# A gated recurrent layer: the first turned inputs by transposing loads instead of TensorE

## The chip, the core and the metric

The kernel runs on one core of a Trainium2 chip. The metric is the device time of one execution in microseconds. The page and the timelines give times from the start of the profiled span. Engines are named as in the profile: PE is TensorE (PEld its weight loads), DVE is VectorE, ACT is ScalarE, POOL is GpSimd, SP is SyncE, which here only issues transfers.

## The reference

```python
def step(h, inp):                       # 128 steps, batch 64, width 512
    x_t, prop = inp
    comb = concatenate([x_t, h], -1)
    z = sigmoid(comb @ Wz + bz)
    r = sigmoid(comb @ Wr + br)
    comb2 = concatenate([x_t, r * h], -1)
    h_cand = tanh(comb2 @ Wh + bh)
    h_new = (1.0 - z) * h + z * h_cand
    h_next = where(prop, tanh(h_new @ Wp + bp), h_new)   # prop: every 4th step
    return h_next, h_new
out = x + (h_new of every step)
```

All is float32. x is 64 x 128 x 512, each gate's weights are 1024 x 512: the upper half meets x, the lower half h.

## The kernel before, in words

**Layout.** The 128 partitions hold two halves of the 512 columns (`s` = 0, 1) for the 64 rows of the batch. A product with a 512 x 512 matrix is four products `k`, each issued once per half: eight matmuls with a stationary operand of 128 x 64 and a moving one of 128 x 256 (`products`, L188). The stationary operand has the contracted columns on the partitions, so h, r*h and x must be turned before they are used.

**A turn on PE** (`turn`, L206 to 222). A float32 is treated as two 16-bit words. For each of two column chunks, four transposes of bf16 halves go to the PSUM tile `turn`, and one copy by DVE or ACT (L204) puts the words side by side again. One step's x takes eight such transposes and two copies (`turn_x`, L237), the copies on ACT.

**A turn by a load.** x of later steps comes in groups `g` of four steps: a load into `xs` (`load_xs`), a copy on POOL that puts the low and high words apart into `xw` (`words_x`, L249, one instruction per step), one transposing load on SP's queue from `xw` to `xv` for the whole group (`planes_x`, L259), and a copy on ACT per step that joins the words in `xT` (`join_x`, L269). In this kernel that begins with group 4, that is with x of step 16. x of steps 0 to 7 comes from `xr`, that of steps 8 to 15 from `early[2]` and `early[3]`, which borrow buffers of the pool `mb` and are loaded at the start.

**The loop over t** (L624) issues, for each step: the R product, sigmoid (L675) and rh = r*h (L676, DVE), the Z product with the turns of rh inside it, z, 1 - z and keep, the H product, tanh (L719), two DVE operations to the new h, and the turns of h. Every fourth step has one more product with Wp and turns `hprop` in place of h. ACT also copies the part that comes from x into the PSUM slot of each gate for the next step (`seed`, L393; L395 in the profile). The program gives each engine its instructions in the order in which the code names them, under a manual schedule, and an engine works through them in that order.

**What fills PE meanwhile.** The products with x do not depend on h. They lie in a list `queue`; `fill(n)` takes n units from it, at places given by hand (`PLACES`, `places`). For x of steps 2 to 7 a unit is a plain product (`plain`, twelve units a step; its result is read by DVE at L420 and L425). From group 2 on the products of eight steps are computed in batches by a fast matrix scheme of 7 x 7 products over sums of x and of weights: `batches`, `batch`, with end copies on ACT (L506, L507, L514) and additions on DVE (L508, L509, L515 to L517), run by `read_out`.

**Sums for the batches.** Sums of weights are made at the start: on DVE `sum_outer` (L311 to L313) in step 0, `sum_outer_1` (L317, two instructions) at the end of step 2, `sum_inner_1` (L325, three instructions) in step 3 ahead of rh, and one more set at the end of step 3 (L320 to L325); the others on POOL. Sums of x are made on POOL: `sum_raw12` and `sum_raw4` (four instructions each), `sum_s12` and `sum_s34` (six each: two for `o`, L352/L353 and L360/L361, and four for `s`, L334 to L337). For group 2, `sum_raw12` stands at the end of step 2, `sum_s12` in step 3 after the R product, `sum_s34` at the end of step 3. POOL also adds h to x for the output in every step (L805).

**Where the turns of x stand in steps 0 to 5.** After the R product x of steps 2, 5, 8, 11, 13, 15 (L663); between fill and the H product in steps 0 to 2 x of 3, 6, 9 (L709); at the end of steps 0 to 4 x of 4, 7, 10, 12, 14 (L755). At two places in a step, after `seed(R, t + 1)` and after keep, stands `join(n)` (L653).

Of the kernel before, what the change touches and what calls it, by code (L numbers as in the profile page):

```python
# [11 lines left out]
U16 = mybir.dt.uint16  # L12
# [5 lines left out]
def kernel(  # L18
# [29 lines left out]
    nc = tc.nc  # L48
# [81 lines left out]
    early = {}  # L130
# [25 lines left out]
    def cut(ps):  # L156
        return ps.rearrange("p (c n) -> p c n", c=C)
# [39 lines left out]
    def product(ps, lT, w, k, start=False):  # L197
        s0, c0 = divmod(k, C)
        products(ps, lT[:, c0, ts(s0, B)], lambda s: w[:, k, ts(s, N)], start)
# [3 lines left out]
    def copy(eng, dst, src):  # L203
        (eng.copy if eng is nc.scalar else eng.tensor_copy)(dst, src)  # L204

    def turn(src, dst, c, name, eng):  # L206


        pt = turn_ps[c][:, :P].bitcast(BF16).rearrange("p (w n) -> p w n", w=2)
        for s in range(S):  # L210
            words = src[:, c * P + s * B : c * P + (s + 1) * B].bitcast(BF16)
            for w in range(2):
                nc.tensor.transpose(  # L213
                    pt[s * B : (s + 1) * B, w, :],
                    words.rearrange("p (n w) -> p w n", w=2)[:, w, :],
                    ident16,
                )
        copy(
            eng,
            dst[:, c, :].bitcast(U16).rearrange("p (n w) -> p n w", w=2),  # L220
            pt.bitcast(U16).rearrange("p w n -> p n w"),
        )
# [6 lines left out]
    xs = {}  # L229
    xw = {}  # L230
    xv = {}

    def new_xT(g):
        if g not in xT:
            xT[g] = xtp.tile([P, Q4, C, P], F32, tag="xT", name=f"xT_{g}")

    def turn_x(t, eng=nc.scalar):  # L237
        g, i = divmod(t, Q4)
        new_xT(g)
        src = xr[g] if g < 2 else early[g]  # L240
        for c in range(C):
            turn(src[:, i, :], xT[g][:, i], c, f"xT_{t}", eng)
# [6 lines left out]
    def words_x(g, i):  # L249

        if g * Q4 >= T:
            return
        if g not in xw:
            xw[g] = one.tile([P, Q4, 2, N], U16, tag="xw", name=f"xw_{g}")
        nc.gpsimd.tensor_copy(
            xw[g][:, i], xs[g][:, i, :].bitcast(U16).rearrange("p (n w) -> p w n", w=2)
        )

    def planes_x(g):  # L259

        if g * Q4 >= T:
            return
        xv[g] = one.tile([P, Q4, 2, C, P], U16, tag="xv", name=f"xv_{g}")
        nc.sync.dma_start_transpose(
            out=xv[g].rearrange("p t w c n -> p (t w c) n"),
            in_=xw[g].rearrange("p t w n -> p (t w n)"),
        )

    def join_x(g, i):  # L269

        if g * Q4 >= T:
            return
        new_xT(g)
        nc.scalar.copy(  # L274
            xT[g][:, i].bitcast(U16).rearrange("p c (n w) -> p w c n", w=2), xv[g][:, i]
        )
# [17 lines left out]
    def inner(i, ka, na):  # L294
        return OPERAND[i](ka)[:, :, :, ts(na, P // 2)]
# [13 lines left out]
    def sum_outer():  # L309
        for ka in range(S):  # L310
            nc.vector.tensor_sub(tw[3][:, ka], outer(1, 1, ka), outer(0, 1, ka))  # L311
            nc.vector.tensor_add(tw[2][:, ka], tw[3][:, ka], outer(0, 0, ka))
            nc.vector.tensor_sub(tw[4][:, ka], outer(1, 0, ka), tw[2][:, ka])  # L313
# [5 lines left out]
    def sum_inner(i, eng):  # L319
        eng.tensor_sub(tt[:, i - 1, 1], inner(i, 1, 1), inner(i, 0, 1))  # L320
        eng.tensor_add(tt[:, i - 1, 0], tt[:, i - 1, 1], inner(i, 0, 0))
        eng.tensor_sub(tt[:, i - 1, 2], inner(i, 1, 0), tt[:, i - 1, 0])

    def sum_inner_1(i, eng):
        eng.tensor_sub(inner(i, 0, 1), inner(i, 0, 1), inner(i, 0, 0))  # L325
# [67 lines left out]
    def seed(i, t):  # L393
        if t < T:
            nc.scalar.copy(cut(slots[i]), G[t][:, :, i, :])  # L395
# [5 lines left out]
    def fill(n):  # L401
        for _ in range(min(n, len(queue))):
            unit, end = queue.pop(0)
            unit()
            if end is not None:
                pending.append(end)

    def read_out():
        while pending:
            pending.pop(0)()  # L410
# [213 lines left out]
    for t in range(T):  # L624
        g, j = divmod(t, Q4)
        prop = j == CHUNK - 1 and t < T - 1
        last = t == T - 1
        pair, u = divmod(t - 3, 8)
# [22 lines left out]
            assert len(queue) == 7  # L651

        def join(n):  # L653
            if pair >= 0 and u in (5, 6):
                join_x(even + 2, 2 * (u - 5) + n)
            elif pair >= 1 and u in (1, 3):
                join_x(odd, u - 1 + n)


        for k in ORDER:  # L660
            product(slots[R], hT, wh[R], k)
        if t < 6:
            turn_x((2, 5, 8, 11, 13, 15)[t])  # L663
        read_out()
        if t == T - 1:
            seed(H_, t)
# [7 lines left out]
        for c in range(C):  # L674
            nc.scalar.activation(act_ps[c], slots[R][:, ts(c, P)], AF.Sigmoid)  # L675
            nc.vector.tensor_mul(rh[:, ts(c, P)], act_ps[c], h[:, ts(c, P)])  # L676
        seed(R, t + 1)
        join(0)


# [12 lines left out]
        nc.scalar.activation(slots[Z], slots[Z], AF.Sigmoid, scale=-1.0)  # L693
        nc.vector.tensor_mul(keep, slots[Z], h)
        join(1)
        seed(Z, t + 1)
        if prop:
# [3 lines left out]
        if t == 0:  # L701
            sum_outer()
            for i in (6, 7, 4):
                sum_inner(i, nc.gpsimd)
                sum_inner_1(i, nc.gpsimd)
        if not thin:
            fill(places[0])
        if t < 3:
            turn_x((3, 6, 9)[t])  # L709


        for k in ORDER:
# [12 lines left out]
            nc.vector.tensor_add(h_new[:, ts(c, P)], pc, keep[:, ts(c, P)])  # L725
        if t < T - 2:
            seed(H_, t + 1)
        read_out()
        fill(places[0] if thin else 5 if places[1] > 6 else 4)
        h = h_new  # L730
# [11 lines left out]
        if prop:  # L742
# [8 lines left out]
            for c in range(C):  # L751
                turn(h, hT, c, f"hpT_{t}", (nc.vector, nc.scalar)[c])
            fill(behind[1] if thin else 2)
        if t < 5:
            turn_x((4, 7, 10, 12, 14)[t])  # L755


        if pair >= 0:
# [37 lines left out]
        if pair >= 0:  # L796
            if u in (1, 2):
                for n in range(2):
                    words_x(even + 2, 2 * (u - 1) + n)
            if u in (5, 6):  # L800
                for n in range(2):
                    words_x(odd + 2, 2 * (u - 5) + n)
# [7 lines left out]
        n = 0  # L810
        if t >= T - CHUNK:
            n = {T - 2: 3, T - 1: 1}.get(t, 0)
        elif j == Q4 - 1:
            n = 4
# [58 lines left out]
```

## Time and profile before

| | |
|---|---|
| median of 3 runs | 1343.7 us (1342.44 to 1344.1) |
| profiled execution, its own time | 1342.88 us |
| its span | 1341.0 us, granted clock 0.998 |
| mean of a turn matmul (L213, from `early`) | 219 ns, 64 of them |
| ACT copy of a turned x (L204), 128x256 uint16 | 375 ns |
| ACT join copy (L274), 128x512 uint16 | 766 ns |
| POOL words copy (L255), 128x512 uint16 | 613 ns |
| transposing loads, issue to landing | 4.3 / 4.3 / 5.0 us (least, median, most of 28) |
| idle of PE waiting for rh | 2.7 us in three places |

A row of a timeline has the start in microseconds, the busy time of the merged instructions, engine, line, operation, output and inputs, count, and in brackets the idle time of the engine before it with what ended it. Successive matmuls overlap in the record, so the time that a row really takes is the distance to the start of the next one.

Steps in the record: step 1 starts at 39.9 us with its R product, step 2 at 56.7, step 3 at 73.5, step 4 at 89.4, step 5 at 99.6, step 6 at 111.1.

### The profile page before, as it was taken

How to read it: one execution, taken by the hardware profiler on the slowest of the kernel's cores; microseconds unless marked ns; L12 is line 12 of the kernel's file. 1: busy time of each engine (PE TensorE's matmuls, PEld its weight loads, DVE VectorE, ACT ScalarE, POOL GpSimd, SP SyncE). 2: the span in 40 equal slices, each digit the busy share in tenths (PEclk: the TensorE clock that was granted, in tenths of full speed). 3: DMA queues.
4: the chain of work that ended last, by engine and by line, in shares of the span. 5: the costliest groups of instructions: out<-in, count | busy, mean ns of one | idle time of the engine just before them, and what ended most of it. 6: DMA issues, size and time to landing. Idle time of an engine off the chain costs nothing.

```text
span 1341.0 us, 37605 instructions
## 1 busy us (share of the span) xinstructions
PE 1329.3 (99%) x15344; PEld 1113.4 (83%) x15344; DVE 702.2 (52%) x1868; ACT 626.6 (47%) x1848; POOL 908.7 (68%) x1111
## 2 busy tenths in 40 slices
PE   9999999999999999999999999999999999999998
PEld 6678888888888888888888888888888888888765
DVE  3355555555555555555555555555555555555444
ACT  1244545454554545455445454545445444554433
POOL 3448776777767777776787767787677687767400
PEclk9999999999999999999999999999999999999999
DMA  9011223122221222213212231222212222131300
GB/s 286 18 33 33 64 47 80 35 49 49 64 65 33 65 42 56 64 33 71 57 34 65 53 76 33 49 48 65 64 33 65 48 49 64 33 80 34 103 18 17
DMA packets 114868, 76.22 MB, mean 57 GB/s; under 512 B 61700, under 2 KB 109956, under 8 KB 114696
## 3 DMA queue, kind: packets, MB, share of 16 engines
q1 hardware_dynamic: 113632, 72.04, 23.2%
q8 instruction: 121, 1.98, 0.6%
q10 hardware_dynamic: 1064, 1.78, 0.4%
q14 instruction: 51, 0.42, 0.1%
HBM read 42.34 MB, written 16.78 MB: 44 GB/s over the span
## 4 chain that ended last, share of the span: by engine, by line
PE 99%; DVE 1%; issue 0%; ACT 0%; POOL 0%; DVEq 0%; POOLq 0%; ACTq 0%
PE rc L188 34%; PE zp L188 20%; PE scratch_q L188 11%; PE scratch_x L188 11%; PE scratch_r L188 10%; PE scratch_a L188 6%; PE turn L213 5%; PE scratch_q L180 0%; PE rc L161 0%; ACT xT L204 0%; PE zp L161 0%; DVE rh L676 0%; DVE turn L720 0%; DVE bias L169 0%; DVE h L725 0%
## 5 line engine op out<-in xcount | busy, mean ns | idle before, releaser
L188 PE MATMUL rc<-wh,rhT 128*64 128x256 f32 x2048 | 245.9, 379 | 0.0
L188 PE MATMUL zp<-wh,hT 128*64 128x256 f32 x1536 | 204.5, 379 | 0.0
L188 PEld LDWEIGHTS rc<-wh,rhT 128*64 128x64 f32 x2048 | 167.4, 137 | 41.1
L544 POOL TENSOR_TENSOR cp<-mb,mb 128x768 f32<-128x768 f32 x72 | 130.8, 1816 | 102.4 <-ACT rc L395 54.8
L188 PE MATMUL rc<-wh,hT 128*64 128x256 f32 x1536 | 186.4, 383 | 0.5
L805 POOL TENSOR_TENSOR xr<-xr,h 128x256 f32<-128x256 f32 x127 | 92.5, 728 | 113.5 <-DVE h L725 112.5
L188 PEld LDWEIGHTS rc<-wh,hT 128*64 128x64 f32 x1536 | 121.9, 137 | 36.5 <-issue 10.4
L544 POOL TENSOR_TENSOR cp<-mb 128x768 f32<-128x768 f32 x44 | 79.9, 1817 | 99.1 <-ACT rc L395 98.0
L720 DVE TENSOR_TENSOR turn<-turn,z 128x128 f32<-128x128 f32 x256 | 75.4, 295 | 129.1 <-ACT turn L719 127.6
L188 PEld LDWEIGHTS zp<-wh,hT 128*64 128x64 f32 x1536 | 119.1, 137 | 24.5
L204 DVE COPY rhT<-turn 128x256 uint16<-128x256 uint16 x256 | 97.6, 420 | 70.2 <-PE turn L213 69.1
L675 ACT ACTIVATE turn<-rc 128x128 f32<-128x128 f32 x256 | 55.4, 261 | 162.7 <-issue 110.1
L204 ACT COPY hT<-turn 128x256 uint16<-128x256 uint16 x127 | 47.3, 372 | 167.7 <-DVE hT L204 127.7
L544 POOL TENSOR_TENSOR mb<-mb,mb 128x768 f32<-128x768 f32 x58 | 105.5, 1820 | 10.7 <-DVE mb L517 10.7
L719 ACT ACTIVATE turn<-rc 128x128 f32<-128x128 f32 x256 | 55.5, 260 | 107.1 <-PE rc L188 107.0
L515 DVE TENSOR_TENSOR mb<-scratch_r,cq 128x384 f32<-128x384 f32 x102 | 56.7, 556 | 89.8 <-ACT cq L514 89.8
L508 DVE TENSOR_TENSOR cx<-scratch_r,cx 128x384 f32<-128x384 f32 x102 | 56.7, 556 | 88.2 <-ACT cx L506 88.2
L395 ACT COPY rc<-cp 128x256 f32<-128x256 f32 x254 | 95.6, 376 | 13.6 <-PE rc L188 1.7
L692 ACT ACTIVATE z<-zp 128x256 f32<-128x256 f32 x128 | 49.0, 383 | 95.1 <-PE zp L188 95.1
L274 ACT COPY xT<-xv 128x512 uint16<-128x512 uint16 x112 | 85.9, 767 | 0.0
L725 DVE TENSOR_TENSOR h<-turn,keep 128x128 f32<-128x128 f32 x254 | 74.1, 292 | 15.7 <-DVE turn L720 0.5
L213 PEld LDWEIGHTS <-h 128*64 128x64 bf16 x1016 | 68.2, 110 | 12.9 <-DVE h L725 4.6
(156 smaller groups left out, 3009.5 us busy)
## 6 DMA issues: line engine op xcount, KB each, us to landing
xr<-in_x_dram SPq DMA_DIRECT2D x62, 256.0 KB, 4.0
out_dram<-xr SPq DMA_DIRECT2D x62, 256.0 KB, 3.3
xs<-in_x_dram SPq DMA_DIRECT2D x56, 256.0 KB, 4.3
wh<-in_L_cond_Wr_dram SPq DMA_DIRECT2D x2, 512.0 KB, 7.7
wh<-in_L_cond_Wz_dram SPq DMA_DIRECT2D x2, 512.0 KB, 8.8
wh<-in_L_cond_Wh_dram SPq DMA_DIRECT2D x2, 512.0 KB, 11.4
early<-in_x_dram SPq DMA_DIRECT2D x4, 256.0 KB, 12.9
wp<-in_L_cond_Wp_dram SPq DMA_DIRECT2D x1, 1024.0 KB
```

What stands on the lines that cost most here:

```text
L188: nc.tensor.matmul(ps[s * B : (s + 1) * B], lhsT=lhs, rhs=rhs(s), start=start, stop=True, skip_group_check=True,)
L204: (eng.copy if eng is nc.scalar else eng.tensor_copy)(dst, src)
L213: nc.tensor.transpose(pt[s * B : (s + 1) * B, w, :], words.rearrange("p (n w) -> p w n", w=2)[:, w, :], ident16,)
L274: nc.scalar.copy(xT[g][:, i].bitcast(U16).rearrange("p c (n w) -> p w c n", w=2), xv[g][:, i])
L395: nc.scalar.copy(cut(slots[i]), G[t][:, :, i, :])
L508: nc.vector.tensor_add(T2[n][:, :nm], r_ps[:, :nm], T2[n][:, :nm])
L515: nc.vector.tensor_add(blocks()[:, :nm, 0, 1], r_ps[:, :nm], q2[:, :nm])
L544: nc.gpsimd.tensor_add(dst, a, b)
L719: nc.scalar.activation(pc, slots[H_][:, ts(c, P)], AF.Tanh)
L720: nc.vector.tensor_mul(pc, pc, z[:, ts(c, P)])
L725: nc.vector.tensor_add(h_new[:, ts(c, P)], pc, keep[:, ts(c, P)])
L805: nc.gpsimd.tensor_add(xr[g][:, j, :], xr[g][:, j, :], h_new)
```

## The change

x of steps 8 to 15 is no longer turned on PE. `words_x` now takes `early[2]` and `early[3]` as sources too, with ACT as the copying engine for these two groups. Two transposing loads (groups 2 and 3) are put on SP's queue, in steps 1 and 2, and eight join copies on ACT, in steps 2 to 4. The turn of x of step 7 moves from the end of step 1 to the place after the R product of step 2. 64 transposes with their weight loads and 16 ACT copies of 128x256 go; eight ACT words copies and eight ACT joins of 128x512 and two transposing loads come. On POOL the instructions and their order stay as they are.

```diff
 def words_x(g, i):
-        nc.gpsimd.tensor_copy(
-            xw[g][:, i], xs[g][:, i, :].bitcast(U16).rearrange("p (n w) -> p w n", w=2)
+        src = (early if g < 4 else xs)[g]
+        copy(
+            nc.scalar if g < 4 else nc.gpsimd,
+            xw[g][:, i],
+            src[:, i, :].bitcast(U16).rearrange("p (n w) -> p w n", w=2),
         )
...
         def join(n):
-            if pair >= 0 and u in (5, 6):
+            if t == 2 and n == 0:
+                join_x(2, 0)
+            elif t in (3, 4):
+                join_x(3, 2 * (t - 3) + n)
+            elif pair >= 0 and u in (5, 6):
                 join_x(even + 2, 2 * (u - 5) + n)
...
-        if t < 6:
-            turn_x((2, 5, 8, 11, 13, 15)[t])
+        if t < 3:
+            turn_x((2, 5, 7)[t])
...
+        if t == 1:
+            for n in range(4):
+                words_x(2, n)
+            planes_x(2)
+        elif t == 2:
+            for n in range(1, 4):
+                join_x(2, n)
+            for n in range(2):
+                words_x(3, n)
         if not thin:
             fill(places[0])
-        if t < 3:
-            turn_x((3, 6, 9)[t])
+        if t < 2:
+            turn_x((3, 6)[t])
...
         if t < T - 2:
             seed(H_, t + 1)
+        if t == 2:
+            for n in range(2, 4):
+                words_x(3, n)
+            planes_x(3)
...
-        if t < 5:
-            turn_x((4, 7, 10, 12, 14)[t])
+        if t == 0:
+            turn_x(4)
```

The first added block stands after the seed of Z, the second after the seed of H.

## The prediction, made before the changed kernel ran

> **What bounds the kernel now.** I read the page's busy shares and chain of waits first: they say whether anything but TensorE (PE) can set the time.
>
> ```profile
> PE 1329.3 (99%) x15344; PEld 1113.4 (83%) x15344; DVE 702.2 (52%) x1868; ACT 626.6 (47%) x1848; POOL 908.7 (68%) x1111
> PE 99%; DVE 1%; issue 0%; ACT 0%; POOL 0%; DVEq 0%; POOLq 0%; ACTq 0%
> ```
>
> PE is the chain almost everywhere. An edit moves the time by the PE slots that it frees, plus the PE idle that it closes, minus the idle that it opens. So the second view is PE's own timeline over loop steps 3 to 5. Columns: start, duration, operation, idle before it; cost is start to start, because durations overlap.
>
> ```profile
> 75.22 0.39 PE L213 MATMUL turn<-ident,early 128*64 128x128 bf16 x8
> 75.45 1.47 PE L188 MATMUL zp<-wh,hT 128*64 128x256 f32 x12
> 76.75 0.50 PE L213 MATMUL turn<-ident,rh 128*64 128x128 bf16 x8
> ...
> 91.11 0.42 PE L213 MATMUL turn<-ident,early 128*64 128x128 bf16 x8
> 91.33 1.50 PE L188 MATMUL zp<-wh,hpT 128*64 128x256 f32 x12
> 93.80 0.51 PE L213 MATMUL turn<-ident,rh 128*64 128x128 bf16 x8 [0.97 <-DVE rh L676]
> ...
> 99.12 0.62 PE L213 MATMUL turn<-ident,early 128*64 128x128 bf16 x8
> 99.55 1.93 PE L188 MATMUL rc<-wh,hT 128*64 128x256 f32 x16
> ...
> 101.50 1.50 PE L188 MATMUL zp<-wh,hT 128*64 128x256 f32 x12
> 104.42 0.51 PE L213 MATMUL turn<-ident,rh 128*64 128x128 bf16 x8 [1.43 <-DVE rh L676]
> ```
>
> Two things are to be seen. The turns of x for one step, eight half-turns, take a slot of 0.23 us, not eight times their mean of 219 ns. And PE waits for rh in steps 4 and 5, but not in step 3, where the turns of rh start exactly 1.30 us after the twelve Z matmuls, their bare length.
>
> The third view is the VectorE (DVE) timeline ahead of rh in step 3, and GpSimd's (POOL) at two places.
>
> ```profile
> 72.19 1.83 DVE L317 TENSOR_TENSOR wx<-wx 128x768 f32<-128x768 f32 x2 [1.27 <-PE scratch_x L188]
> 73.94 0.68 DVE L420 TENSOR_TENSOR cp<-scratch_a,bias 128x512 f32<-128x512 f32 x1
> 74.54 0.41 DVE L425 TENSOR_TENSOR cp<-scratch_x,bias 128x256 f32<-128x256 f32 x1
> 74.87 1.49 DVE L325 TENSOR_TENSOR wx<-wx 128x384 f32<-128x384 f32 x3
> 76.40 0.49 DVE L676 TENSOR_TENSOR rh<-turn,h 128x128 f32<-128x128 f32 x2
> ```
>
> ```profile
> 33.28 1.78 POOL L320 TENSOR_TENSOR tt<-tw 128x384 f32<-128x384 f32 x1 [6.91 <-DVE tw L312]
> ...
> 69.80 0.74 POOL L805 TENSOR_TENSOR xr<-xr,h 128x256 f32<-128x256 f32 x1 [1.01 <-issue]
> 76.28 0.73 POOL L352 TENSOR_TENSOR o<-xT 128x256 f32<-128x256 f32 x1 [5.74 <-ACT xT L204]
> ```
>
> From 72.19 DVE is full up to rh, and rh's start at 76.40 plus 0.35 (0.33 and 0.34 at the two waits) is just when PE takes it. POOL is idle in that stretch because o waits for the turn of x step 11; it starts when DVE is through.
>
> **The change, part by part.**
>
> *Turns gone.* Eight slots, start to start: steps 8 to 15 give 0.22, 0.23, 0.23, 0.23, 0.22, 0.22, 0.43 and 0.23, together 2.01 us. The 0.43 at 99.12 is a slot that also waited for its PSUM tile, from which ScalarE (ACT) was still copying hT until 99.38. The turn of step 7 only moves into the place of step 8's.
>
> *Waits in steps 4 and 5.* On ACT the copies of turns 13 and 15 wait for PE to pass the R product; behind them stand the copies of the finished batch (L506, L507 at 91.99; L514 at 102.15), then the sigmoid, and DVE's additions of the batch stand ahead of rh. With the turns gone the batch copies run as soon as ACT has copied hpT or hT (89.11, 99.38), before the R product ends. So rh follows R directly, as in step 6: R starts at 111.14, its sigmoid at 113.18, and the Z matmuls run from 112.89 to the turns at 114.19, with no idle. Z to turns takes 2.47 and 2.92 us in steps 4 and 5; without the wait 1.30. Gains: 1.17 and 1.62 us.
>
> *Step 3's cover.* Two slots go ahead of L317 (the end of step 1 and turn 9), so PE and DVE both come 0.46 us earlier. Turns 10 and 11 go behind the point that releases L317: 0.46 more for PE alone. PE would be ready at 76.75 - 0.92 = 75.83, rh at 76.40 - 0.46 + 0.35 = 76.29. A wait of 0.46 opens: those two turns give nothing.
>
> *Moved POOL work.* In the changed program o of group 2 waits only for joins that ACT finishes near 64. POOL goes from the addition to xr (now about 69.35) straight into the twelve instructions of the sums s12 and s34. In the old run they took 76.28 to 83.0, 6.7 us; now about 70.0 to 76.7. That is on top of L317 (now 71.73) and the three L325. What does the overlap cost? The nearest row is L320: beside DVE's L313 (33.23, 0.96 us, both inputs in SBUF) it took 1.78 us where its fellows take 1.00, so POOL stood still for nearly all of the DVE instruction. No row shows DVE blocked by POOL. Here the Trainium skill, page "SBUF — State Buffer", section "Who interferes with whom", speaks against the change: a VectorE instruction with two SBUF inputs and a GpSimd instruction that reads SBUF exclude each other for a whole instruction, whichever came first. L317 and L325 have two SBUF inputs; L420, L425 and rh read PSUM for one. By the row alone, DVE loses nothing; by the rule, each of the five DVE instructions can find a POOL instruction in its way. If the two take turns, with POOL holding about 0.35 us for 128x128 (0.46 in all) and 0.63 for 128x256 (0.73 in all), I get delays of 0.22, 0.26, 0.44, 0.58 and 0.28: 1.78 us, an estimate from these rows and that page, all on rh and so on PE. Low end 0 (a DVE gain is excluded: PE's release sets L317's start). High end 5.0: DVE stands until POOL's chain ends at 76.7. I take 1.78.
>
> *ACT's added work.* Eight words copies and eight joins for sixteen turn copies. The join's row is 0.77 us, start to start 0.62 (138.05 to 138.67); POOL's words copy is 0.61; I take 0.62 for both. Step 1: four copies in the idle from 45.69 to 49.45 (2.5 of 3.76). Step 2: three joins and two words copies from 62.2 to tanh at 67.7 (3.1 of 5.5), then two more before the hT copy (1.2 of 2.0). Behind each are tanh and the hT copy, for which PE would wait. Up to 0.94 us each costs nothing; at twice my value, 1.24, the first batch delays only copies of x, the others cost about 0.7 and 0.5. Joins in steps 3 and 4 stand where later steps have them (ahead of z, and ahead of Z's seed), without PE idle there.
>
> *The loads.* SP's queue is empty from 28.5 to 90.35, so the two transposing loads delay nothing. All 28 of the old run land in 4.3 to 5.0 us. The second starts near 69.9 and lands by 74.9; its join stands after the seed at 75.6, and z behind that needs ACT at 77.2. Slack is 1.7 us or more. The early loads of x were over by 38.5.
>
> *Kept.* The 0.39 us wait at 86.96 for L515 has its DVE queue unchanged, and POOL is through by then.
>
> Sum: 2.01 + 1.17 + 1.62 - 0.46 - 1.78 = 2.56 us. The profiled execution took 1342.88 us around a span of 1341.0; it would take 1340.3. The median shown is 1343.7, so I forecast 1341.1.
>
> **The rivals.** A measurement of this kernel can tell about 0.2%, 2.7 us, from no change; 1341.0 is that bound.
>
> *Forecast, shared access costs 1 to 2.4 us:* 1340.4 to 1341.8. For: the rule and L320's row. Chance 0.45.
>
> *DVE keeps the access* (0 to 0.8 us): gain 3.5 to 4.3, time 1339.4 to 1340.2. For: the only collision on record ended for DVE. Chance 0.30.
>
> *DVE starved* (2.4 to 5.0): time 1341.8 to 1344.3. For: POOL's instructions follow each other without a gap (78.85, 79.26, 79.68). Against: dependent ones leave gaps (77.09 to 77.90 for 0.73). Chance 0.12.
>
> *The waits of steps 4 and 5 stay,* because a batch's additions are late for another reason: 2.01 - 0.46 - 1.78 is nothing gained, 1343.9 (1342.2 without the lock). Against: step 6 shows the same order without a wait. Chance 0.08.
>
> *Slower: the transposing load is late.* The Trainium skill, "VectorE: DVE Perf Modes", section "The three transpose paths", gives 1309 ns for a 128x128 block by DMA against 390 on TensorE, and so speaks against this change: 16 blocks one after another would be 20.9 us, landing at 90.8. By the row it is 4.3. The join would hold z and tanh in step 3; ACT has about 3 us of room to tanh, so every microsecond of flight beyond some 8 is lost, and the kernel is slower by 2.7 us once a load takes about 13. By the page it would be about 10 us slower, 1354. The row decides; chance 0.05.
>
> **The numbers.** The first two and the lower half of the third are held by 1339.2 to 1343.0. Faster: all of the second (0.30) and 0.18 of the first, 0.48. Slower 0.05. Within 0.2%: 0.47.
>
> **What would show it.** No turns of early; PE without idle before the rh turns of steps 4 and 5; an idle of 0.5 to 2.5 us before those of step 3, put down to rh; L317 and L325 on DVE, or the POOL instructions beside them, longer than 0.96, 0.55 and 0.46 us; both transposing loads landing within 5 us. A wait of ACT for xv, or of PE for tanh in steps 1 to 3, would prove me wrong; so would step 3's wait above 3 us.

## The result, and the profile after

The changed kernel takes 1341.47 us (median of 19 runs, 1339.89 to 1343.18) against 1343.7 us for the kernel before (19 runs, 1342.44 to 1345.63). The ratio is 0.9983, 95% interval 0.9977 to 0.9990: a small gain, near 0.2% and too close to it to say on which side. The forecast was 1341.1. Ratios here compare executions at a granted clock near 1; a single one of those below, of late joins with a tile of its own, ran at 0.752 and took 1733.16 us, and is left out of its ratio.

The profile page's busy shares and chain hardly differ from those before, so the stages must be read one by one.

```profile
span 1339.4 us, 37483 instructions
PE 1328.2 (99%) x15280; PEld 1112.5 (83%) x15280; DVE 704.0 (53%) x1868; ACT 630.7 (47%) x1848; POOL 912.0 (68%) x1111
PE 98%; DVE 1%; issue 0%; ACT 0%; POOL 0%; DVEq 0%; POOLq 0%; ACTq 0%
```

PE has 64 matmuls less and is busy 1.1 us less, and the span is 1.6 us shorter. The two spans are not the best measure, though: step 1 begins at 39.92 us before and at 41.21 after, while the program is the same up to there. From step 1's R product to step 6's, where all of the change lies, PE takes 71.22 us before (111.14 - 39.92) and 68.30 after (109.51 - 41.21): 2.92 us less. That stretch is used below beside the ratios. It is read from one execution of each kernel, but it repeats where programs agree: step 1 takes 16.56 us in the changed kernel, in *group 2 only* and in *late joins* below, which share it.

PE's timeline after the change, steps 3 to 5, at the places that were shown before:

```profile
74.11 1.90 PE L188 MATMUL rc<-wh,hT 128*64 128x256 f32 x16
75.84 1.47 PE L188 MATMUL zp<-wh,hT 128*64 128x256 f32 x12
79.16 0.51 PE L213 MATMUL turn<-ident,rh 128*64 128x128 bf16 x8 [1.85 <-DVE rh L683]
...
93.30 1.49 PE L188 MATMUL zp<-wh,hpT 128*64 128x256 f32 x12
94.59 0.42 PE L213 MATMUL turn<-ident,rh 128*64 128x128 bf16 x8
...
101.59 1.49 PE L188 MATMUL zp<-wh,hT 128*64 128x256 f32 x12
102.88 0.42 PE L213 MATMUL turn<-ident,rh 128*64 128x128 bf16 x8
```

The waits of steps 4 and 5 are gone: from Z to the turns of rh it takes 1.29 us in both, where it took 2.47 and 2.92. In step 3, which had no wait, it takes 3.32 us: a new wait of 2.02 us. DVE and POOL in front of it, first DVE:

```profile
73.03 2.30 DVE L320 TENSOR_TENSOR wx<-wx 128x768 f32<-128x768 f32 x2 [1.27 <-PE scratch_x L188]
75.26 0.68 DVE L423 TENSOR_TENSOR cp<-scratch_a,bias 128x512 f32<-128x512 f32 x1
75.86 0.41 DVE L428 TENSOR_TENSOR cp<-scratch_x,bias 128x256 f32<-128x256 f32 x1
76.19 2.71 DVE L328 TENSOR_TENSOR wx<-wx 128x384 f32<-128x384 f32 x3
78.83 0.48 DVE L683 TENSOR_TENSOR rh<-turn,h 128x128 f32<-128x128 f32 x2
```

```profile
72.94 0.45 POOL L337 TENSOR_TENSOR s<-o 128x128 f32<-128x128 f32 x1
73.47 1.05 POOL L338 TENSOR_TENSOR s<-s,o 128x128 f32<-128x128 f32 x1
74.49 1.17 POOL L339 TENSOR_TENSOR s<-o 128x128 f32<-128x128 f32 x1
75.61 0.46 POOL L340 TENSOR_TENSOR s<-o,s 128x128 f32<-128x128 f32 x1
76.03 0.73 POOL L363 TENSOR_TENSOR o<-xT 128x256 f32<-128x256 f32 x1
76.72 1.04 POOL L364 TENSOR_TENSOR o<-xT,o 128x256 f32<-128x256 f32 x1
77.84 0.65 POOL L337 TENSOR_TENSOR s<-o 128x128 f32<-128x128 f32 x1
78.57 0.65 POOL L338 TENSOR_TENSOR s<-s,o 128x128 f32<-128x128 f32 x1
```

The DVE lines are those that were L317, L420, L425, L325 and L676 before. The two L320 take 2.30 us in place of 1.83, the three L328 2.71 in place of 1.49; L423 and L428, which read PSUM for one input, stay at 0.68 and 0.41 though POOL works beside them. On POOL the 128x128 instructions swell from 0.46 to as much as 1.17 where L320 or L328 runs; L340 at 75.61, beside L423 and L428, keeps its 0.46. No row behind L320's start has an idle time in brackets: both engines' instructions are simply longer.

### The profile page after: what moved, and what is told of

Same layout as the page of the kernel before. It is cut to its first block, busy times and chain, and to the rows that moved or that the text cites. A ratio compares the mean times of both kernels' runs of the same rounds, so it can differ in the third digit from the quotient of the medians.

```text
span 1339.4 us, 37483 instructions
## 1 busy us (share of the span) xinstructions
PE 1328.2 (99%) x15280; PEld 1112.5 (83%) x15280; DVE 704.0 (53%) x1868; ACT 630.7 (47%) x1848; POOL 912.0 (68%) x1111
## 3 DMA queue, kind: packets, MB, share of 16 engines
q10 hardware_dynamic: 1064, 1.78, 0.4%
## 4 chain that ended last, share of the span: by engine, by line
PE 98%; DVE 1%; issue 0%; ACT 0%; POOL 0%; DVEq 0%; POOLq 0%; ACTq 0%
PE rc L188 34%; PE zp L188 20%; PE scratch_q L188 11%; PE scratch_x L188 11%; PE scratch_r L188 10%; PE scratch_a L188 7%; PE turn L213 5%; PE scratch_q L180 0%; DVE wx L328 0%; DVE wx L320 0%; PE zp L161 0%; PE rc L161 0%; DVE turn L736 0%; DVE bias L169 0%; DVE cp L423 0%
## 5 line engine op out<-in xcount | busy, mean ns | idle before, releaser
L518 DVE TENSOR_TENSOR mb<-scratch_r,cq 128x384 f32<-128x384 f32 x102 | 56.7, 556 | 87.0 <-ACT cq L517 87.0
L277 ACT COPY xT<-xv 128x512 uint16<-128x512 uint16 x120 | 91.5, 765 | 0.0
```

The lines of the kernel that those rows point to most:

```text
L277: nc.scalar.copy(xT[g][:, i].bitcast(U16).rearrange("p c (n w) -> p w c n", w=2), xv[g][:, i])
L518: nc.vector.tensor_add(blocks()[:, :nm, 0, 1], r_ps[:, :nm], q2[:, :nm])
```

## The experiments

**Halves of the change.** *Group 3 only* leaves x of steps 8 to 11 on PE, *group 2 only* leaves x of steps 12 to 15 there. The cut below shows where the turns stand; the copies, the load and the joins of the group that stays on PE are taken out as well.

```diff
 # group 3 only, against the changed kernel
-        if t < 3:
-            turn_x((2, 5, 7)[t])
+        if t < 4:
+            turn_x((2, 5, 8, 11)[t])
...
-        if t < 2:
-            turn_x((3, 6)[t])
+        if t < 3:
+            turn_x((3, 6, 9)[t])
...
-        if t == 0:
-            turn_x(4)
+        if t < 3:
+            turn_x((4, 7, 10)[t])
 # group 2 only, against the changed kernel
-        if t < 3:
-            turn_x((2, 5, 7)[t])
+        if t < 6 and t != 3:
+            turn_x((2, 5, 7, 0, 13, 15)[t])
...
-        if t == 0:
-            turn_x(4)
+        if t in (0, 3, 4):
+            turn_x({0: 4, 3: 12, 4: 14}[t])
```

> Only x of steps 12 to 15 (group 3) by the transposing load; x of steps 8 to 11 stays on TensorE at its old places, so the POOL sums s12 and s34 of group 2 start at their old place, behind DVE's chain of step 3. Theory (the gain lies in steps 4 and 5, the loss in the collision of POOL and DVE in step 3): the four turn slots of group 3 (1.1 us) and the waits of steps 4 and 5 (2.8) go, step 3 keeps its bare 1.30 us from Z to the turns of rh: about 3.9 us below before, ratio 0.9971, better than the whole change. Rival (the gain comes in equal parts from all eight turns, the loss from ACT's added copies): about half of the whole change, ratio 0.9991.

> Only x of steps 8 to 11 (group 2) by the transposing load; x of steps 12 to 15 stays on TensorE at its old places. Theory: four slots go (0.9 us), the waits of steps 4 and 5 stay, and in step 3 the wait for rh opens to about 2.0 us because POOL's sums s12 and s34 lie on DVE's L320 and L328: about 1.1 us above before, ratio 1.0008. Rival (half of the whole change): ratio 0.9991, with the waits of steps 4 and 5 shorter.

Group 3 only: ratio 0.9968 (0.9957 to 0.9979), steps 1 to 6 in 67.18 us, 4.04 less than before. Group 2 only: 1.0013 (1.0004 to 1.0022), 72.34 us, 1.12 more. The two parts add up to the whole: -4.04 + 1.12 = -2.92. So the change is a good half and a bad half, and the half that pays is the one that changes neither L317 nor the start of POOL's sums. PE's lines of group 2 only, steps 3 to 5:

```profile
78.95 0.51 PE L213 MATMUL turn<-ident,rh 128*64 128x128 bf16 x8 [1.85 <-DVE rh L681]
96.00 0.50 PE L213 MATMUL turn<-ident,rh 128*64 128x128 bf16 x8 [0.97 <-DVE rh L681]
106.62 0.51 PE L213 MATMUL turn<-ident,rh 128*64 128x128 bf16 x8 [1.43 <-DVE rh L681]
```

The old waits of 0.97 and 1.43 us stand beside the new one of 1.85. In group 3 only, L320 and L328 are back at 1.83 and 1.49 us, and POOL's first `o` starts at 76.95, as the last of them ends (77.03).

**The waits of steps 4 and 5 without any transposing load.** One edit in the kernel before puts the batch's copies and additions ahead of the turn of x:

```diff
+        if t in (4, 5):
+            read_out()
         if t < 6:
             turn_x((2, 5, 8, 11, 13, 15)[t])
         read_out()
```

> The kernel before, all x turned on TensorE, with one edit: in steps 4 and 5 the batch copies and additions are issued ahead of the turn of x, so on ACT they stand in front of the turn copies instead of behind them. Theory (the waits of steps 4 and 5 are a matter of the order on ACT and DVE, not of the turns on PE): both waits close, 2.8 us faster, ratio 0.9979, more than the whole change. Rival (the turns themselves hold up rh): the waits stay, ratio 1.0000.

Ratio 0.9974 (0.9962 to 0.9986); 68.46 us from step 1 to step 6, 2.76 less, with all 64 turns still on PE. PE in step 4, from Z to the turns of rh, is without idle, 1.32 us in place of 2.47 (in step 5 1.32 in place of 2.92):

```profile
91.26 1.50 PE L188 MATMUL zp<-wh,hpT 128*64 128x256 f32 x12
92.58 0.50 PE L213 MATMUL turn<-ident,rh 128*64 128x128 bf16 x8
```

ACT's timeline in the same step:

```profile
89.43 0.65 ACT L204 COPY xT<-turn 128x256 uint16<-128x256 uint16 x2 [0.39 <-PE turn L213]
89.96 0.50 ACT L506 COPY cx<-scratch_x 128x384 f32<-128x384 f32 x1
90.33 0.51 ACT L507 COPY cq<-scratch_q 128x384 f32<-128x384 f32 x1
91.38 0.65 ACT L204 COPY xT<-turn 128x256 uint16<-128x256 uint16 x2 [0.54 <-PE turn L213]
91.91 0.45 ACT L677 ACTIVATE turn<-rc 128x128 f32<-128x128 f32 x2
```

The batch copies now lie in the time in which ACT used to wait for PE, and the sigmoid comes 0.74 us earlier after the start of R (89.30 to 91.91, against 89.38 to 92.73 before). The waits were a matter of what stood in front of rh in the engines' queues, as the prediction has it, and most of what the change brings in its good half is to be had by moving one call.

**The collision without the loads.** In the kernel before, the turns of steps 9 to 11 are moved ahead within step 2, so that POOL's sums can start before L317 (their old places, after the R product of step 3 and at the end of step 2, fall away):

```diff
...
-        if not thin:
+        if t == 2:
+            fill(6)
+            turn_x(9)
+            fill(6)
+        elif not thin:
             fill(places[0])
         if t < 3:
-            turn_x((3, 6, 9)[t])
+            turn_x((3, 6, 10)[t])
...
+        if t == 2:
+            turn_x(11)
...
```

> The kernel before, all x still turned on TensorE, with the turns of steps 9, 10 and 11 moved earlier within step 2, so that POOL's sums s12 start in front of L317, without any transposing load or words copy on ACT. Theory: the collision comes all the same, DVE's stretch from L317 to rh grows from 4.2 to 5.8 us; with the two slots that now lie ahead of L317 the wait for rh in step 3 is about 2.0 us, and the kernel is 2.0 us slower than before, ratio 1.0015. Rival (the loads or ACT's copies lengthen DVE's instructions): the stretch stays 4.2, the wait is 0.5, ratio 1.0003.

Ratio 1.0029 (1.0019 to 1.0039), slower than expected; steps 1 to 6 take 74.69 us, 3.47 more than before. The stretch from L317 to rh grew from 4.21 to 5.47 us (75.70 to 81.17), and in step 3 PE takes 3.00 us from Z to the turns of rh, a wait of 1.70:

```profile
75.70 2.67 DVE L317 TENSOR_TENSOR wx<-wx 128x768 f32<-128x768 f32 x2 [1.35 <-PE scratch_x L188]
78.29 0.68 DVE L420 TENSOR_TENSOR cp<-scratch_a,bias 128x512 f32<-128x512 f32 x1
78.89 0.41 DVE L425 TENSOR_TENSOR cp<-scratch_x,bias 128x256 f32<-128x256 f32 x1
79.22 2.03 DVE L325 TENSOR_TENSOR wx<-wx 128x384 f32<-128x384 f32 x3
...
81.50 0.51 PE L213 MATMUL turn<-ident,rh 128*64 128x128 bf16 x8 [1.53 <-DVE rh L676]
```

There is no transposing load and no words copy by ACT in that part of the run, so neither makes DVE longer; POOL's place in time does. It cost 1.26 us and not 1.6; POOL was further on, and had only two 128x128 instructions left (79.18 and 79.60) when DVE came to L325 at 79.22. Most of the rest of the slowdown is my own edit: turn 11 had to wait 1.15 us and 0.23 us for DVE's L729, which reads the PSUM tile `turn` that turn 11 writes.

**The loads without the collision.** The whole change, with the joins of x of steps 10 and 11 put behind the sigmoid of step 3. Each join of group 3 moves one place later, and `sum_s12` is issued behind the joins that it needs:

```diff
             if t == 2 and n == 0:
                 join_x(2, 0)
+            elif t == 3 and n == 0:
+                join_x(2, 2)
+                join_x(2, 3)
-            elif t in (3, 4):
-                join_x(3, 2 * (t - 3) + n)
+            elif t in (3, 4, 5) and 2 * (t - 3) + n - 1 < 4:
+                join_x(3, 2 * (t - 3) + n - 1)
...
```

> The whole change, but the joins of x of steps 10 and 11 stand in step 3 behind the sigmoid, and those of group 3 one place later each, so POOL cannot start s12 before DVE is through with L328. Nothing else moves. Theory (POOL and DVE exclude each other): DVE's stretch from L320 to rh shrinks from 5.8 us to its 4.2 of before, the wait for rh in step 3 from 2.0 to about 0.5, and the time falls by 1.6 us under the whole change, ratio to before about 0.9970. Rival (DVE's instructions are longer for another reason: SBUF traffic of the transposing loads or of ACT's copies): the stretch stays near 5.8 and the ratio near 0.9983.

Half of that came true. L320 and L328 are 1.83 and 1.49 us again, rh's wait shrank to 0.31 us, but the ratio is 0.9990 (0.9981 to 0.9999). PE waited 1.99 us for L509. ACT shows what came instead:

```profile
78.76 0.38 ACT L704 ACTIVATE zp<-zp 128x256 f32<-128x256 f32 x1
82.84 0.76 ACT L277 COPY xT<-xv 128x512 uint16<-128x512 uint16 x1 [3.71 <-DMA xv<-xw]
83.47 0.40 ACT L398 COPY zp<-cp 128x256 f32<-128x256 f32 x1
83.91 0.38 ACT L709 COPY zp<-bias 128x256 f32<-128x256 f32 x1
84.22 0.47 ACT L509 COPY cx<-scratch_x 128x384 f32<-128x384 f32 x1
```

`xv` has one buffer. The second load had to wait until the late joins had read the first, and started at 78.33 in place of 70.91. The join that needs it held ACT for 3.71 us, the batch copies behind it (L509) came late (84.22 in place of 82.10), and PE waited for them. This is much like the prediction's slower rival, brought about by hand: a load that lands near 82.8 in place of 75 costs 2.0 us, on PE's wait for a batch copy. The join that waits stands behind z here, and ahead of z in the changed kernel, so the place of the loss there is not shown. A tile of its own for group 2's turned words mends it:

```diff
-        xv[g] = one.tile([P, Q4, 2, C, P], U16, tag="xv", name=f"xv_{g}")
+        xv[g] = one.tile([P, Q4, 2, C, P], U16, tag="xv" if g != 2 else "xv_first", name=f"xv_{g}")
```

> As the kernel with late joins, with a tile of its own for the turned group 2, so that the second transposing load need not wait until the late joins have read the first. Theory (in the kernel with late joins only that wait took the place of the collision): the second load starts near 71 again, ACT does not wait for it, the stretch from L320 to rh stays at about 4.1 us, and the time is 4.3 us below before, ratio 0.9968. Rival (late joins are themselves too much for ACT in step 3): PE still waits some 2 us for the batch copies, ratio 0.999.

Ratio 0.9968 (0.9956 to 0.9980), steps 1 to 6 in 66.67 us, 4.55 less than before. L320 and L328 stay at 1.83 and 1.48 us:

```profile
72.80 1.83 DVE L320 TENSOR_TENSOR wx<-wx 128x768 f32<-128x768 f32 x2 [1.28 <-PE scratch_x L188]
...
75.47 1.48 DVE L328 TENSOR_TENSOR wx<-wx 128x384 f32<-128x384 f32 x3
```

Without the collision the whole change is worth what its turns and the two waits are worth.

**A version meant to beat both.** Two more waits were left: 0.31 us for rh in step 3 and 0.47 us (0.63 start to start) for L518.

```diff
...
+        if t == 3:
+            fill(2)
         rhT = new_T("rhT", f"rhT_{t}")
...
-            sum_inner(5, nc.vector)
+            nc.vector.tensor_sub(tt[:, 4, 1], inner(5, 1, 1), inner(5, 0, 1))
             sum_inner_1(5, nc.vector)
...
             read_out()
+            if t == 3:
+                nc.vector.tensor_add(tt[:, 4, 0], tt[:, 4, 1], inner(5, 0, 0))
+                nc.vector.tensor_sub(tt[:, 4, 2], inner(5, 1, 0), tt[:, 4, 0])
```

> A version meant to beat both: the late joins with the separate tile, two units of the queue in front of the turns of rh in step 3, and of the sums for weight 5 only the two instructions that the next products need ahead of L518, the other two behind the batch's additions. Theory: besides the 4.3 us, the 0.3 us wait for rh in step 3 and the 0.55 us wait for L518 close: about 5.1 us below before, ratio 0.9962. If the two waits move to another place instead, as the kernel with late joins alone, 0.9968.

Ratio 0.9959 (0.9947 to 0.9972), but PE's stretch is 66.90 us: nothing won over 66.67. Both waits closed, and a new one of 1.12 us for the turned hprop opened. DVE:

```profile
85.54 0.54 DVE L772 TENSOR_TENSOR tt<-tt,wx 128x384 f32<-128x384 f32 x1
86.11 2.06 DVE L773 TENSOR_TENSOR tt<-wx,tt 128x384 f32<-128x384 f32 x1
88.09 0.41 DVE L204 COPY hpT<-turn 128x256 uint16<-128x256 uint16 x1
```

and POOL beside it:

```profile
85.69 2.06 POOL L551 TENSOR_TENSOR mb<-mb,bias 128x768 f32<-128x768 f32 x1 [1.89 <-DVE mb L520]
87.71 1.04 POOL L833 TENSOR_TENSOR xr<-xr,h 128x256 f32<-128x256 f32 x1
```

L773 takes 2.06 us where its neighbour takes 0.54. L551 began before it (85.69) and ended at 87.75; L773 ended at 88.17, 0.42 us behind that. This fits a DVE instruction that stands until POOL's is through, the row that the trace of before lacked. The same two sums behind the copies of the turned hprop:

> The filled version once more, with the two deferred sums for weight 5 behind the copies of the turned hprop instead of in front of them. Theory (there the second of them, L773, met POOL's 128x768 addition of the bias and took 2.06 us in place of 0.56, and the hprop copy behind it held PE for 1.1 us): the wait for hprop goes, no other comes, and the stretch from step 1 to step 6 on PE falls from 66.9 to about 65.7 us, the time to 5.5 us below before, ratio 0.9959. If the deferred sums now hold up rh of step 4 in the same way, PE waits there and the ratio stays near 0.9968.

The wait for hprop is gone and no other came, though the two sums still meet POOL (0.87 and 0.97 us): nothing waits for them there. PE takes 65.56 us from step 1 to step 6, 5.66 less than before. The ratio is 0.9966 (0.9953 to 0.9978; medians 1338.06 and 1343.29 us). The intervals of this version, of the last one and of late joins with a tile of its own overlap. All three lie clear of the kernel before; against the changed kernel (0.9977 to 0.9990) only that of the version just before this one is clear (0.9947 to 0.9972), the other two overlap it at the edge, and only PE's timeline ranks the three.

## Why the prediction was right

The forecast, 1341.1 us, was for a gain of 2.56 us; the ratio makes it 2.3 us (1343.7 times 0.0017), with 1.3 to 3.1 inside its interval, and PE's stretch 2.92. The interval is too wide to test the terms; the stretch does, and there the sum is 0.36 too small. The collision and the lost cover cost 0.22 less than estimated, a term of 0.22 was left out (below), and some 0.1 went the other way.

*Turns gone, 2.01 us.* Held. Steps 1 and 2 show it alone: 16.79 us each before, 16.56 and 16.34 after, that is 0.23 and 0.45 less for one slot and two.

*Waits of steps 4 and 5, 1.17 and 1.62 us.* Held: 2.47 and 2.92 us from Z to the turns became 1.29. That the cause is the order on ACT and DVE is shown by the kernel that only issues the batch's reads first. A further 0.11 us came in each step, which the sum left out: before, the turns of rh start (93.80) ahead of the end of DVE's second half of rh (93.94) and take 0.33 us to the next Z matmuls at 94.13; after, rh is through at 94.31 and they take 0.22 (94.59 to 94.81).

*Step 3's lost cover, 0.46 us.* Held in kind: without the collision, Z to turns is 1.61 us, a wait of 0.31. DVE's stretch from L320 to rh is 4.08 us there in place of 4.21, which is most of the difference.

*POOL's sums on DVE's chain, 1.78 us in a range of 0 to 5.0.* Held, with 1.59 us (L320 to rh: 5.80 in place of 4.21), or 1.72 against the 4.08 of late joins with a tile of its own. The five instructions were 0.22, 0.25, 0.43, 0.53 and 0.25 us longer (1.18, 1.21, 0.98, 1.08 and 0.80 us, against 0.96 and 0.55), where the prediction had 0.22, 0.26, 0.44, 0.58 and 0.28. So the estimate was right piece by piece, and not only in its sum. Three pieces of evidence meet: with POOL early and no load the delay is there (1.26 us), with the loads and POOL late it is gone, and of the DVE instructions in the same stretch those with one PSUM input are not touched. The rule that the prediction takes from the Trainium skill ("SBUF — State Buffer", section "Who interferes with whom") agrees with all three. The wait in step 3 came to 2.02 us against 2.24.

*ACT's added copies.* Nothing was lost, as forecast; the words copies took less than assumed (four in 2.17 us, 0.52 start to start in place of 0.62).

*The loads.* They started at 49.11 and 70.91 and none of the 30 took more than 4.8 us. The 1309 ns for a block that the prediction quotes from the Trainium skill ("VectorE: DVE Perf Modes", section "The three transpose paths"), taken 16 times in a row, would have made it slower; the measured 4.2 to 4.8 us for 16 blocks does not agree with that reading, and the old trace's 4.3 us was the right row. What a late load costs was seen in the first kernel with late joins. For a landing 12 us after the usual start the prediction's working gives some 4 us, lost at tanh; there it was 2.0, at the batch copy. As the join stands one place later there, this speaks against the working but does not measure it.

Of the rivals, "DVE keeps the access" and "DVE starved" fall: both engines lost time, DVE 1.59 us and POOL 2.0 (its twelve sums took 8.72 us, 71.32 to 80.04, in place of 6.71), and 1.59 lies between their ranges, 0 to 0.8 and 2.4 to 5.0. "The waits stay" falls with 1.29.

What I did not settle: whether the two engines take strict turns. An estimate from turns fits each of the five DVE instructions to 0.05 us, but the records show only longer instructions, not who held what.

## What to carry to other kernels

Ask of work that is freed from a gate when it will run instead: here POOL's sums lost the copy that had held them back, started 5 us earlier (71.32 in place of 76.28) and ran onto the one stretch in which DVE had no slack. And before moving work to another engine or queue, look whether the wait that it would end is only an order of instructions on an engine: one call moved ahead brought 2.76 us, the eight steps of turns moved away 2.92. A buffer that is single is part of the schedule; a later reader delays the next transfer.

## What the runs showed of the hardware that I had not expected

- The delay works in both directions: L773 on DVE took 2.06 us, in place of 0.54, beside a POOL instruction that takes 1.82 by itself, and L320 on POOL took 1.78 beside a DVE one of 0.96. A single meeting of a short DVE instruction with a long POOL one costs as much as five meetings with short ones (1.5 and 1.59 us).
- Identical starts of a program differ: step 1 began at 39.92 in one profiled execution and at 41.21 in another, with the same instructions up to there. The granted clock between 12 and 16 us was 0.78 in the first and 0.50 in the second, and closely spaced x matmuls (about 0.22 us for two instead of 0.43) began near 13.5 and near 16 us. The run times, too, lie in groups some 1.3 us apart. Across the ten profiled executions nine agree: clocks of 0.78 to 0.85 there go with starts at 39.63 to 39.92, 0.61 with 40.59, 0.50 to 0.52 with 40.97 to 41.25. The tenth, of early sums, shows a clock of 1.00 and a start at 41.21, with the wide spacing up to about 14.5, so the clock record alone does not settle the cause, and what sets the start was not tested. The scatter is as large as half of the effect studied, so stretches of PE's timeline told the versions apart better than whole runs.
